# Outer-product rows on one Trainium2 core: a round of 256 adjacent batch rows, with all input loaded at the start

## The chip, the cores and the metric

The kernel runs on one core of a Trainium2 chip. The metric is the device time of one execution in microseconds (us), given as the median of several runs. Of the core's engines three matter here: VectorE (DVE in the profile) and ScalarE (ACT), which compute, and SyncE (SP), whose queue issues every transfer to the core's 16 DMA engines. The on-chip memory has 128 partitions, and a tile has one line in each.

## The reference

For each of 4096 batch rows of 256 numbers, all products of two of the row's numbers are wanted, each pair once:

```python
r_inputs: (4096, 256) float32

dot = jnp.einsum('bi,bj->bij', inputs, inputs)
iu, ju = jnp.triu_indices(d)
return dot[:, iu, ju]
```

The output has 4096 rows of 256 x 257 / 2 = 32,896 numbers (131,584 bytes a row, 539 MB in all). The input is 4.2 MB.

## The kernel before

The 4096 batch rows are worked on in 16 rounds (`groups`) of 256 rows, two rows (`REPEAT`) on each of the 128 partitions. Before the change partition p owns the 32 adjacent batch rows 32p to 32p+31, and round g takes rows 32p+2g and 32p+2g+1 from each partition (`x_in` and `x_out`). In memory the rows of neighbouring partitions are thus 32 x 131,584 bytes = 4.2 MB apart in the output.

The whole input stays in one tile `xt`, with 32 rows on each partition. It is loaded in pieces by `load` (L111 to L113), on SyncE's queue: round 0 alone (256 KB), then rounds 1 to 6 (1.5 MB), then three rounds at a time (768 KB each), called after the first piece of rounds 3, 6 and 9 (the last two lines of the loop). In the memory a partition's piece of a load is one run: 2 KB, 12 KB and 6 KB. The layer that places instructions need not keep the order of the source: the profile has the load for rounds 7 to 9 at 7.62 us, the other two at 467.5 and 706.1 us.

Within a round the 32,896 output columns are cut into five pieces of equal size (`PIECES`, in units of 64 columns). For each piece a tile `o` is taken from a pool of three (`opool`), filled and stored. A piece is a list of segments, one for each i: x[i] times x[j], for a run of j. A few of the longest go to ScalarE (L129, one instruction per row), the others to VectorE (L138, both rows in one instruction). Then SyncE issues two stores (L145), one per row, each of 128 partitions x 26,368 bytes (26,112 for the first piece of a round). The first piece of round 0 is cut into four smaller ones (`FIRST`), so that storing starts early. A tile can be filled again when both stores of the tile three pieces earlier have landed.

SyncE's queue holds loads and stores in one order: an instruction that waits there holds back those behind it.

Of the kernel before, what the change touches and what calls it, by code (L numbers as in the profile page):

```python
# [1 line left out]

# [4 lines left out]

F32 = mybir.dt.float32
AF = mybir.ActivationFunctionType
ALU = mybir.AluOpType  # L10

P = 128
UNIT = 64
REPEAT = 2
PIECES = 5
BUDGET = 0.95
AHEAD = 7
LOADED = 3
FIRST = [512, 1536, 3584]


def even_borders(lo: int, hi: int, pieces: int) -> list[int]:
    units = (hi - lo) // UNIT
    return [lo + units * c // pieces * UNIT for c in range(pieces)] + [hi]


def runs(d: int, lo: int, hi: int) -> list:


    found, at = [], 0  # L30
    for i in range(d):
        a, b = max(at, lo), min(at + d - i, hi)
        if a < b:
            found.append((i, i + a - at, a, b - a))
        at += d - i
    return found


def vector_ops(block: list) -> list:

    ops, k = [], 0
    while k < len(block):
        i, j, at, n = block[k]
        m = 2 if k + 2 < len(block) and i == j else 1
        ops.append((block[k], m))
        k += m
    return ops  # L50


def interleave(block: list) -> list:


    half = len(block)
    while half and len(vector_ops(block[:half])) > len(vector_ops(block[half:])):
        half -= 1
    a, b = vector_ops(block[:half]), vector_ops(block[half:])
    return [op for k in range(max(len(a), len(b))) for ops in (a, b) for op in ops[k : k + 1]]  # L60


def vector_time(block: list) -> float:
    return sum(68 + 1.046 * REPEAT * n * m for (*_, n), m in vector_ops(block))


def split(block: list, budget: float) -> int:


    scalar, k = 0.0, 0  # L70
    while k < len(block):
        scalar += REPEAT * (184 + 0.837 * block[k][3])
        if vector_time(block[k:]) <= budget or scalar > vector_time(block[k + 1 :]):
            break
        k += 1
    return k


def window(ap: bass.AP, free: list) -> bass.AP:
    return bass.AP(ap.tensor, ap.offset, [list(ap.ap[0]), *free])  # L80


@with_exitstack
def kernel(
    ctx: ExitStack, tc: tile.TileContext, x: bass.AP, out: bass.AP
):

    nc = tc.nc
    n, d = x.shape
    width = out.shape[1]
    assert n % (P * REPEAT) == 0 and width == d * (d + 1) // 2 and width % UNIT == 0
    groups = n // (P * REPEAT)
    borders = even_borders(0, width, PIECES)
    slot = max(b - a for a, b in zip(borders, borders[1:]))

    xpool = ctx.enter_context(tc.tile_pool(name="x", bufs=1))  # L100
    opool = ctx.enter_context(tc.tile_pool(name="o", bufs=3))

    x_in = x.rearrange("(p r) d -> p (r d)", p=P)
    x_out = out.rearrange("(p g r) c -> g p r c", p=P, r=REPEAT)


    total = n // P * d
    xt = xpool.tile([P, total + 1], F32, name="x")
    nc.vector.memset(xt[:, total:], 0.0)  # L109

    def load(g: int, end: int):  # L111
        a, b = g * REPEAT * d, end * REPEAT * d
        nc.sync.dma_start(xt[:, a:b], x_in[:, a:b])  # L113

    load(0, 1)
    load(1, AHEAD)

    for g in range(groups):
        for c, (lo, hi) in enumerate(zip(borders, borders[1:])):
            o = opool.tile([P, REPEAT, slot], F32, tag="o", name=f"o_{g}_{c}")  # L120
            first = g == c == 0
            cuts = [lo, *(FIRST if first else []), hi]
            for a, b in zip(cuts, cuts[1:]):
                block = runs(d, a, b)
                k = split(block, 0.0 if first else BUDGET * REPEAT * (b - a))
                for i, j, at, length in block[:k]:
                    for r in range(REPEAT):
                        row = (g * REPEAT + r) * d
                        nc.scalar.activation(  # L129
                            o[:, r, at - lo : at - lo + length],  # L130
                            xt[:, row + j : row + j + length],
                            AF.Copy,
                            scale=xt[:, row + i : row + i + 1],
                        )
                row = g * REPEAT * d
                for (i, j, at, length), m in interleave(block[k:]):
                    at -= lo
                    nc.vector.tensor_tensor(  # L138
                        o[:, :, at : at + m * length],
                        window(xt[:, row + j :], [[d, REPEAT], [1, m], [1, length]]),  # L140
                        window(xt[:, row + i :], [[d, REPEAT], [1, m], [0, length]]),
                        ALU.mult,
                    )
                for r in range(REPEAT):
                    nc.sync.dma_start(x_out[g][:, r, a:b], o[:, r, a - lo : b - lo])  # L145
            if c == 0 and g and g % LOADED == 0 and g - LOADED + AHEAD < groups:
                load(g - LOADED + AHEAD, min(g + AHEAD, groups))


# [1 line left out]
_INS = ["r_inputs"]  # L151
_OUTS = [((4096, 32896), "float32")]


# [20 lines left out]
```

## Time and profile before

Nine runs have a median of 1279.27 us (1278.96 to 1279.62). The profiled execution took 1279.17 us; its span, from the first to the last instruction, is 1277.4 us.

| what | value | read from |
|---|---|---|
| profiled execution, and its span | 1279.17 us, 1277.4 us | times, page |
| VectorE busy, instructions | 995.9 us (78%), 1813 | page, part 1 |
| ScalarE busy, instructions | 486.6 us (38%), 1547 | page, part 1 |
| bytes read from and written to memory | 4.19 MB, 538.97 MB | page, part 3 |
| stores of 3,296 KB and 3,264 KB | 128 and 30 issues | page, part 6 |
| loads | five: 256 KB, 1,536 KB and three of 768 KB | page, part 6 |
| VectorE waiting for stores to land | 205.5 us in 62 waits | waits |

The page divides the span into 40 equal slices and gives for each the busy share of the engines, the busy share of the 16 DMA engines in tenths (9 is 90% or more), and the GB/s that they moved. The chain of waits goes back from the last instruction to what released each step. A view by stretches gives the same for any stretch of time. Under the page lie the packet records: start, duration and size of each of the 24,624 packets that the queue's transfers were split into. A packet carries one partition's run, and 128 partitions are shared out as eight packets to each of the 16 engines.

### The profile page before, as it was taken

How to read it: one execution, taken by the hardware profiler on the slowest of the kernel's cores; microseconds unless marked ns; L12 is line 12 of the kernel's file. 1: busy time of each engine (PE TensorE's matmuls, PEld its weight loads, DVE VectorE, ACT ScalarE, POOL GpSimd, SP SyncE). 2: the span in 40 equal slices, each digit the busy share in tenths (PEclk: the TensorE clock that was granted, in tenths of full speed). 3: DMA queues.
4: the chain of work that ended last, by engine and by line, in shares of the span. 5: the costliest groups of instructions: out<-in, count | busy, mean ns of one | idle time of the engine just before them, and what ended most of it. 6: DMA issues, size and time to landing. Idle time of an engine off the chain costs nothing.

```text
span 1277.4 us, 3976 instructions
## 1 busy us (share of the span) xinstructions
DVE 995.9 (78%) x1813; ACT 486.6 (38%) x1547; POOL 0.2 (0%) x4
## 2 busy tenths in 40 slices
DVE  8997887887878777788788768788787777777770
ACT  6523434243342523424334243342523425234250
POOL 0000000000000000000000000000000000000000
DMA  8999999999999999999999999999999999999997
GB/s 357 435 428 430 435 423 434 430 426 435 427 430 431 426 434 412 429 434 432 435 432 427 422 422 433 433 431 432 433 429 434 431 427 434 429 429 433 426 433 323
DMA packets 24655, 543.43 MB, mean 425 GB/s; under 512 B 2736, under 2 KB 2736, under 8 KB 3760
## 3 DMA queue, kind: packets, MB, share of 16 engines
q1 hardware_dynamic: 24624, 543.17, 99.5%
q14 instruction: 31, 0.25, 0.0%
HBM read 4.19 MB, written 538.97 MB: 425 GB/s over the span
## 4 chain that ended last, share of the span: by engine, by line
DMA 70%; DVE 25%; SPq 1%; issue 1%; DVEq 0%
DMA out_dram<-o 70%; DVE o L138 25%; SPq L145 1%; DMA x<-in_r_inputs_dram 0%; DVEq L138 0%
## 5 line engine op out<-in xcount | busy, mean ns | idle before, releaser
L138 DVE TENSOR_TENSOR o<-x 128x356 f32<-128x356 f32 (+61 forms) x1812 | 995.8, 632 | 245.0 <-DMA out_dram<-o 205.5
L129 ACT ACTIVATE o<-x 128x253 f32<-128x253 f32 (+41 forms) x1546 | 485.3, 404 | 753.6 <-DMA out_dram<-o 744.1
L129 ACT ACT_TABLE_LOAD x1 | 1.3, 1283 | 0.7 <-PEq L162 0.7
L109 DVE MEMSET x<- 128x1 f32 x1 | 0.1, 59 | 0.8 <-PEq L162 0.8
L162 POOL MEMSET const-bfloat16-1.0<- 128x1 bf16 x1 | 0.1, 101 | 0.0
L162 POOL MEMSET const-uint8-127<- 128x1 uint8 x1 | 0.1, 101 | 0.0
L162 POOL MEMSET const-float32-0.0<- 128x1 f32 x1 | 0.1, 98 | 0.2 <-issue 0.2
L162 POOL MEMSET const-float32-1.0<- 128x1 f32 x1 | 0.1, 98 | 0.0
## 6 DMA issues: line engine op xcount, KB each, us to landing
out_dram<-o SPq DMA_DIRECT2D x128, 3296.0 KB, 29.6
out_dram<-o SPq DMA_DIRECT2D x30, 3264.0 KB, 28.6
out_dram<-o SPq DMA_DIRECT2D x2, 1472.0 KB, 11.1
x<-in_r_inputs_dram SPq DMA_DIRECT2D x3, 768.0 KB, 36.1
out_dram<-o SPq DMA_DIRECT2D x2, 1024.0 KB, 7.8
x<-in_r_inputs_dram SPq DMA_DIRECT2D x1, 1536.0 KB, 6.1
out_dram<-o SPq DMA_DIRECT2D x2, 512.0 KB, 3.8
out_dram<-o SPq DMA_DIRECT2D x2, 256.0 KB, 3.3
```

Source lines behind the costliest of these rows:

```text
L109: nc.vector.memset(xt[:, total:], 0.0)
L129: nc.scalar.activation(o[:, r, at - lo : at - lo + length], xt[:, row + j : row + j + length], AF.Copy, scale=xt[:, row + i : row + i + 1],)
L138: nc.vector.tensor_tensor(o[:, :, at : at + m * length], window(xt[:, row + j :], [[d, REPEAT], [1, m], [1, length]]), window(xt[:, row + ...
L145: nc.sync.dma_start(x_out[g][:, r, a:b], o[:, r, a - lo : b - lo])
L162: nc = _bacc.Bacc("TRN2", target_bir_lowering=False, num_devices=1)
```

## The change

A round becomes a stretch of 256 adjacent batch rows: round g holds rows 256g to 256g+255, and partition p holds rows 256g+2p and 256g+2p+1. The rows that neighbouring partitions write are then 2 x 131,584 bytes = 263 KB apart. In the input a round's 2 rows of a partition are one run of 2 KB, and different rounds of a partition are no longer adjacent. The input is loaded by three transfers ahead of the loop: round 0, rounds 1 to 7, and rounds 8 to 15. `load` and its calls in the loop go, with their constants.

```diff
-AHEAD = 7
-LOADED = 3
...
-    x_in = x.rearrange("(p r) d -> p (r d)", p=P)
-    x_out = out.rearrange("(p g r) c -> g p r c", p=P, r=REPEAT)
+    x_in = x.rearrange("(g p r) d -> p g (r d)", p=P, r=REPEAT)
+    x_out = out.rearrange("(g p r) c -> g p r c", p=P, r=REPEAT)
...
-    def load(g: int, end: int):
-        a, b = g * REPEAT * d, end * REPEAT * d
-        nc.sync.dma_start(xt[:, a:b], x_in[:, a:b])
-
-    load(0, 1)
-    load(1, AHEAD)
+    cuts = [0, 1, groups // 2, groups]
+    for a, b in zip(cuts, cuts[1:]):
+        xs = xt[:, a * REPEAT * d : b * REPEAT * d]
+        nc.sync.dma_start(xs.rearrange("p (g c) -> p g c", g=b - a), x_in[:, a:b])
...
-            if c == 0 and g and g % LOADED == 0 and g - LOADED + AHEAD < groups:
-                load(g - LOADED + AHEAD, min(g + AHEAD, groups))
```

## The prediction

> **What bounds the kernel.** I read the slices of the span first, then the queues and the chain, then the waits, then short stretches where the DMA rate dips.
>
> ```profile
> span 1277.4 us, 3976 instructions
> ...
> DVE 995.9 (78%) x1813; ACT 486.6 (38%) x1547; POOL 0.2 (0%) x4
> ...
> DMA  8999999999999999999999999999999999999997
> GB/s 357 435 428 430 435 423 434 430 426 435 427 430 431 426 434 412 429 434 432 435 432 427 422 422 433 433 431 432 433 429 434 431 427 434 429 429 433 426 433 323
> ...
> q1 hardware_dynamic: 24624, 543.17, 99.5%
> ...
> HBM read 4.19 MB, written 538.97 MB: 425 GB/s over the span
> ...
> DMA 70%; DVE 25%; SPq 1%; issue 1%; DVEq 0%
> ```
>
> The 16 DMA engines are busy from the second slice to the last but one, and nearly all bytes are output. VectorE is idle for a fifth of the span, so its 25% in the chain is time the DMA is working too. The queue's own waits say the same: SyncE mostly waits for VectorE to have something to store, while VectorE in turn waits for a store to free a buffer.
>
> ```profile
> SPq L145 <- DVE o L138: 1101.0, 83, 16.8
> ...
> DVE o L138 <- DMA out_dram<-o: 205.5, 62, 5.7
> ```
>
> So the end is set by how long the DMA engines need for their packets plus the time they stand empty. A store that VectorE finishes earlier buys nothing. The stretches show where the DMA falls below its usual rate (the last two columns are the share of the 16 engines that is busy and GB/s; a share above 1 comes from counting a packet where it starts).
>
> ```profile
> 4.00:24.00 20.00, 20.00 (x28) 15.21 (x43) 0.00 (x0) 1.00 1.00 397
> 24.00:28.00 4.00, 4.00 (x7) 0.69 (x3) 0.00 (x0) 1.00 0.56 238
> 28.00:68.00 40.00, 40.00 (x89) 20.35 (x69) 0.00 (x0) 1.00 1.01 432
> ...
> 488.00:512.00 24.00, 19.17 (x30) 6.94 (x22) 0.00 (x0) 1.00 1.01 411
> ...
> 728.00:752.00 24.00, 19.50 (x31) 6.43 (x20) 0.00 (x0) 1.00 1.01 408
> ...
> 1268.00:1276.00 8.00, 0.00 (x0) 0.00 (x0) 0.00 (x0) 1.00 0.18 76
> ```
>
> Four places lose time: the start; a hole at 24 to 28 us, where the stores of the first tile are through and the next tile's are issued only at 26.27 us; and two dips, at the loads that SyncE issues at 467.5 and 706.1 us, whose packets run some 30 us later. In the tail a few engines finish 6 to 7 us after the rest (the packet records show three, ending at 1274.5, 1274.9 and 1276.0 us, the others at 1268.5 to 1269.4).
>
> **The change part by part.** Durations are of the profiled execution, 1277.4 us of span and 1279.17 us in all; the median is 0.10 us above that.
>
> *Mid-run loads go.* The two dips cost (1 - 411/432) x 24 = 1.17 us and (1 - 408/432) x 24 = 1.33 us: their bytes are counted in the GB/s, so this is pure loss, from reads between writes. The packet records agree: 26,112-byte stores there take 1.6 to 2.0 us instead of a median 0.971. Gain 2.5 us. The two loads also leave SyncE's queue, where they hold 1.24 and 1.26 us in time in which SyncE waits for VectorE anyway; worth nothing while that wait lasts (16.8 us at its longest), and if that cover were gone 2.5 us. The third load (rounds 7 to 9) was issued at 7.62 us already, so "the last nine rounds" is six in the trace: 1.5 MB that really move.
>
> *All loads first, in 2 KB packets.* A round's rows are now 2 KB per partition in memory, so rounds 1 to 15 take 15 x 8 = 120 packets of 2 KB per engine in place of 8 of 12 KB and 24 of 6 KB. In the first load a 2 KB packet follows the one before it by 80 ns once the engine is running (84 ns long, overlapping), a 12 KB one by 457, a 6 KB one takes 234 (230 with the same overlap). So 120 x 80 = 9.6 us against 8 x 457 + 24 x 230 = 9.2: loss 0.4 us. Less mixing at the start: now loads end, then stores begin, one border instead of two or three; half of one dip's two borders is 0.6 us, today's packets before 24 us carry 1.4 us per engine over their medians, of which 0.4 is the latency of the first loads and stays. I take a gain of 0.4, with bounds of 0 and 1.0.
>
> *The hole fills.* Loads would be through at about 2.7 (first load landed) + 9.6 = 12.3 us. Behind them lie the stores of the first tile, 6.7 MB or 15.5 us at 432 GB/s, so the engines work until 27.8 us, past 27.1 us where the packets of the next tile's stores begin today. Gain 0.44 x 4 = 1.76 us. By engine the hole is 0.45 to 2.6 us in the packet records; the engine that ends last decides, so these are the bounds. What is late next: the first tile's buffer comes free about 1.5 us later, but VectorE wants it only after its third tile (stored at 38.6 us), 10 us of cover; without that cover VectorE would start late by that 1.5 us, and the DMA still would not run dry, having two tiles queued.
>
> *Issue on SyncE.* Two loads of 896 and 1024 packets now stand before the first store, ready at 4.81 us. No row has such an issue. A 128-packet one takes 0.38 to 0.42 us on an empty queue and up to 1.26 us on a full one. If it grows with packets, that is 15 x 0.42 = 6.3 us (SyncE free at 7.4) or 15 x 1.26 = 18.9 (free at 20.0). VectorE and ScalarE depend on the first load alone and keep computing. I take the short end, since these are issued on an empty queue, as its row is: nothing lost, for the load packets run until 12.3 us.
>
> *Addresses.* Neighbouring partitions write 263 KB apart instead of 4.2 MB, with the same packets: 16,384 of 26,368 bytes, 3,840 of 26,112. Per engine that is 1,024 and 240. The trace has no other spacing, so the price is bounded by its rows. Medians are 978 and 971 ns, means 982.4 and 979.9, so today's disturbance is 4.4 x 1,024 + 8.9 x 240 = 6.6 us. If the new spacing removed it: -6.6 us. If every packet took what the slowest tenth takes today (989 and 981): 13.7 - 6.6 = +7.0 us. If stores ran as the mixed stretch at 411 GB/s does: 5% or some 60 us. I take 0: the nearest row is the same store at its usual pace, 978 ns with 975 the shortest, which looks like the engines' own limit rather than the memory's.
>
> The Trainium skill has a rule that speaks against the change. "DMA: Bandwidth & Descriptors", section Latency and other measured facts, reports copies slowed by power-of-two spacing of partition rows: full speed (214 GB/s each way) at 4 MiB plus 4 KiB, 103 at plain 4 MiB, 207 at 512 KiB, and a pad of 192 bytes not helping. The spacing before is 4 MiB plus 16 KiB, and its 978 ns agree with full speed; the new one is 256 KiB plus 1 KiB, which the page does not have. By its nearest line, 207 of 214, the stores would take 3.4% longer, an estimate of about +42 us and 1317 in place of the sum below.
>
> *Unchanged:* computing, store count, the three late engines of the tail.
>
> Sum: -2.5 + 0.4 - 0.4 - 1.8 + 0 = -4.3 us. 1279.17 - 4.3 = 1274.9; the median's 0.1 us does not matter. That is -0.34%; about 0.2%, or 2.6 us, can be told from no change.
>
> **The rivals.**
>
> *Stores get slower by their spacing.* Place: every 26 KB packet. 4.3 us over 1,264 packets is 3.4 ns: a mean of 985.8 ns for the large ones gives the whole gain back, and beyond 987.9 ns the kernel is slower by over 0.2%. With all packets at today's slowest tenth the time is 1274.9 + 7.0 = 1281.9. For it: the margin is tiny, and in the stretch from 30 to 480 us, where the engines run most in step, packets exceed the median by 2.6 us per engine, against 0.2 us from 505 to 700. Against: the packets sit at one duration in all rounds.
>
> *The issue holds the first stores.* SyncE free at 20.0 us, stores done 15.5 us later at 35.5 in place of 27.1: +8.4, less the 3.7 us of load time that no longer comes later (16 packets x 230 ns) and the 2.5 of the dips: +2.2, 1281.4. For it: 1.2 us issues are common. Against: in the trace those come with several transfers queued ahead.
>
> *The gain is hidden.* The engine that ends last had the smallest hole (0.45 us), and mixing at the start grows to what one dip costs (1.3 lost in place of 0.4 gained): -2.5 + 0.4 + 1.3 - 0.45 = -1.3, 1277.9, no change. For it: only the last engine counts. Against: the three late ones fell behind gradually, after the hole.
>
> *Spacing helps.* Today's disturbance goes too: 1274.9 - 6.6 = 1268.3. For it: quiet stretches exist. Against: nothing ties them to addresses.
>
> **How the numbers follow.** Forecast 0.42; spacing helps 0.09; hidden 0.10; issue 0.09 (0.04 of it within 0.2%); slower stores 0.30 (0.03 of it within 0.2%). Faster 0.51, same 0.17, slower 0.32. The forecast's own range is 1273.5 to 1276.6 by the bounds of hole and mixing. The range runs from 1269, leaving out some 0.05 of the helped cases, to 1290, 12 ns more per packet than forecast, leaving out about half of the slower stores, 0.15.
>
> **What would show it.** No dips in mid-run and no hole at 24 to 28 us; three input issues before the first store; input packets over by 13 us; large packets still at 978 ns median and 982 mean; the tail as before. Wrong if that mean is above 986, if the first store's packets start after 14 us with idle engines before them, or if VectorE waits for anything but stores.

## The result, and the profile after

The changed kernel takes 1275.13 us (median of 10 runs, 1274.73 to 1276.16), the kernel before 1279.19 us. The ratio is 0.9969, with a 95% interval from 0.9961 to 0.9976: faster by 4.1 us, or 0.3%. The forecast was 1274.9 us.

The page of the changed kernel, its slices, queue, bytes and chain:

```profile
span 1273.1 us, 3975 instructions
...
DVE 996.1 (78%) x1813; ACT 486.7 (38%) x1547; POOL 0.2 (0%) x4
...
DMA  9999999999999999999999999999999999999998
GB/s 380 431 432 434 425 435 425 436 424 435 428 433 425 434 425 435 424 435 426 435 427 432 429 431 425 435 428 431 428 433 428 432 430 431 425 434 426 435 426 353
...
q1 hardware_dynamic: 26000, 543.17, 99.8%
...
HBM read 4.19 MB, written 538.97 MB: 427 GB/s over the span
...
DMA 70%; DVE 25%; issue 1%; SPq 1%; DVEq 0%
```

It is the same kernel with the same bound: the same bytes, the same chain, the DMA engines full. What is gone is the 412 GB/s slice of before, and the first slice moves 380 instead of 357 GB/s. The stretches in which before lost time (columns as before: stretch, length, busy time by engine, clock, DMA share, GB/s):

```profile
4.00:24.00 20.00, 18.52 (x26) 15.40 (x44) 0.00 (x0) 1.00 1.02 401
24.00:28.00 4.00, 4.00 (x7) 0.00 (x0) 0.00 (x0) 1.00 1.02 436
28.00:68.00 40.00, 40.00 (x89) 21.05 (x70) 0.00 (x0) 1.00 1.01 434
488.00:512.00 24.00, 20.87 (x32) 8.75 (x27) 0.00 (x0) 1.00 1.02 437
728.00:752.00 24.00, 19.09 (x32) 5.78 (x18) 0.00 (x0) 1.00 1.02 437
1264.00:1272.00 8.00, 0.00 (x0) 0.00 (x0) 0.00 (x0) 1.00 0.36 155
```

The hole at 24 to 28 us (0.56 of the engines busy before) is full, and both dips (411 and 408 GB/s before) are at 437. In the first line VectorE has lost 1.48 us of work, which it had not lost before; its rows in order of time (start, length, what, and in brackets the idle time ahead of it and what ended that):

```profile
3.62 4.28 DVE L133 TENSOR_TENSOR o<-x 128x512 f32<-128x512 f32 x9 [2.76 <-DMA x<-in_r_inputs_dram]
9.38 50.72 DVE L133 TENSOR_TENSOR o<-x 128x988 f32<-128x988 f32 x84 [1.48 <-DMA x<-in_r_inputs_dram]
```

In round 0 VectorE waits twice for input: for round 0's own load, and at 7.9 us for the second load, whose last engine lands at 9.35 us. The source of the second wait is in the code: where one instruction covers two segments (m = 2), the second is one number shorter but is read at full length, so it reads one number past the end of its row, which behind a partition's second row is round 1's first. The instruction that waits (the first of the 128x988 group, 2 x 2 x 247 numbers) is the first of round 0 with m = 2. Before, the load with round 1 had landed at 7.25 us, in time.

Where the 4.3 us of span went is best read round by round, in one profile of each kernel. In the records each store has 16 landings, one per DMA engine. They do not name the engines: below, the last engine is the one that lands last, and the middle engine is the median of the 16. From the landing of a round's last store on the last engine to that of the round before (us; round 0 from the start of the span):

| kernel | round 0 | round 6 | round 9 | rounds 7, 8 and 10 | end |
|---|---|---|---|---|---|
| before | 91.00 | 82.44 | 82.31 | 78.50, 78.55, 77.70 | 1276.40 |
| changed | 93.13 | 78.53 | 78.59 | 78.72, 78.84, 78.45 | 1272.20 |

Round 0 is 2.1 us longer, since it now has all input; rounds 6 and 9 are 3.9 and 3.7 us shorter, their input and dips being gone; of these 7.6 us, 1.25 are given back in rounds 7, 8 and 10 (0.75 of it in round 10, which was quicker than the usual 78.5 before). The other rounds differ by 0.05 us in sum. 2.13 - 7.63 + 1.25 + 0.05 = -4.20, of the 4.3 us of span.

### The profile page after: what moved, and what is told of

Read it like the earlier page. It is cut to its first block, busy times and chain, and to the rows that moved or that the text cites. A ratio compares the mean times of both kernels' runs of the same rounds, so it can differ in the third digit from the quotient of the medians.

```text
span 1273.1 us, 3975 instructions
## 1 busy us (share of the span) xinstructions
DVE 996.1 (78%) x1813; ACT 486.7 (38%) x1547; POOL 0.2 (0%) x4
## 4 chain that ended last, share of the span: by engine, by line
DMA 70%; DVE 25%; issue 1%; SPq 1%; DVEq 0%
DMA out_dram<-o 70%; DVE o L133 25%; SPq L140 1%; DMA x<-in_r_inputs_dram 1%; DVEq L133 0%; SPq L111 0%
## 6 DMA issues: line engine op xcount, KB each, us to landing
x<-in_r_inputs_dram SPq DMA_DIRECT2D x1, 2048.0 KB, 13.5
out_dram<-o SPq DMA_DIRECT2D x2, 512.0 KB, 11.1
out_dram<-o SPq DMA_DIRECT2D x2, 256.0 KB, 10.6
```

## The experiments

**Spacing and load time apart.** The change does two things at once: it spreads stores differently, and it moves the loads. Three kernels fill the square.

The changed loads with the old spacing:

```diff
-    x_out = out.rearrange("(g p r) c -> g p r c", p=P, r=REPEAT)
+    x_out = out.rearrange("(p g r) c -> g p r c", p=P, r=REPEAT)
```

> The changed kernel with one line put back: the stores go to the old addresses, 4.2 MB apart per partition, while the input stays as changed. The products of each row are unchanged, but they are written to other rows of the output, so only the spacing of the stores differs from the changed kernel. Theory A (the time of the loads is everything, the spacing nothing): 1275.1 us within 0.5, an undisturbed round 78.33 us between the median landings of its last stores, 26,368-byte packets at a median of 978 to 981 ns. Theory B (the new spacing brings part of the gain): slower than the changed kernel by 1 us or more, 1276 to 1279, with more excess per packet. Theory C (the new spacing costs something that the loads' gain covers): faster than the changed kernel, 1271 to 1274.

Measured: 1274.95 us (1274.79 to 1275.01), ratio to before 0.9967 [0.9954, 0.9979]. Large packets have a median of 982 ns (981 in the changed kernel) and a mean of 983.9 (983.7). Going from 4.2 MB to 263 KB is worth nothing either way. Theory A.

The old rows and spacing with all input first:

```diff
-    load(1, AHEAD)
+    load(1, groups // 2)
+    load(groups // 2, groups)
...
-            if c == 0 and g and g % LOADED == 0 and g - LOADED + AHEAD < groups:
-                load(g - LOADED + AHEAD, min(g + AHEAD, groups))
```

> The kernel before with one thing changed: all input is loaded ahead of the loop in three transfers (rounds 0, 1 to 7, 8 to 15), rows and spacing as before, so that a partition's piece of a load is one run of 2, 14 or 16 KB. Theory A: the whole gain and a little more, since large packets cost 0.4 us less: 1274.7 us, rounds 6 and 9 at 78.3 us instead of 81, no hole at 24 to 28 us. Theory B: part of the gain is missing, 1276 to 1279.

Measured: 1274.22 us (1274.16 to 1274.35), ratio 0.9961 [0.9948, 0.9975]. Theory A. This is the change without its new rows, and it is the fastest kernel of this study that computes the whole result. A second set of runs:

> The kernel with all input loaded first and old rows and spacing once more, to set it against the changed kernel's 1275.1 us with more runs: 1274.2 us again if its 0.9 us are real; 1275 us if the first five runs were lucky. Theory for the difference: input packets of 14 and 16 KB cost 0.4 us less than those of 2 KB, and the loads land 0.6 to 1.2 us sooner.

Measured: 1274.26 us (1274.19 to 1274.37), ratio 0.9962 [0.9950, 0.9975]; the slowest of its ten runs is below the fastest of the changed kernel (1274.73). In the first set's profile its input lands on the last engine at 13.98 us instead of 15.13.

The new rows and spacing with the loads at their old times:

```diff
+AHEAD = 7
+LOADED = 3
...
-    cuts = [0, 1, groups // 2, groups]
-    for a, b in zip(cuts, cuts[1:]):
+    def load(a: int, b: int):
         xs = xt[:, a * REPEAT * d : b * REPEAT * d]
         nc.sync.dma_start(xs.rearrange("p (g c) -> p g c", g=b - a), x_in[:, a:b])
+    load(0, 1)
+    load(1, AHEAD)
...
+            if c == 0 and g and g % LOADED == 0 and g - LOADED + AHEAD < groups:
+                load(g - LOADED + AHEAD, min(g + AHEAD, groups))
```

> The changed kernel's rows and spacing with the loads at the times of the kernel before (rounds 0, 1 to 6, then three rounds at a time in mid-run). Theory A: as the kernel before plus some 0.2 us for the smaller packets, 1279.4 us, with rounds 6 and 9 at 81 us and the hole at 24 to 28 us. Theory B: faster than the kernel before by 1 us or more though the loads stay in mid-run, 1275 to 1278.

Measured: 1279.87 us (1279.59 to 1280.54), ratio 1.0006 [0.9997, 1.0015]: as before, 0.5 us above theory A's 1279.4. The hole and the dips are back; its stretches:

```profile
24.00:28.00 4.00, 4.00 (x7) 0.38 (x2) 0.00 (x0) 1.00 0.64 270
488.00:512.00 24.00, 19.12 (x30) 7.48 (x23) 0.00 (x0) 1.00 1.02 410
728.00:752.00 24.00, 19.45 (x30) 7.09 (x22) 0.00 (x0) 1.00 0.99 399
```

and the same stretches with the old rows and all input first (its second set of runs):

```profile
24.00:28.00 4.00, 4.00 (x6) 0.00 (x0) 0.00 (x0) 1.00 0.99 424
488.00:512.00 24.00, 20.87 (x32) 8.27 (x26) 0.00 (x0) 1.00 1.00 429
728.00:752.00 24.00, 18.08 (x30) 5.79 (x18) 0.00 (x0) 1.00 1.00 428
```

| | loads in mid-run | all loads first |
|---|---|---|
| rows 4.2 MB apart, large input packets | 1279.19 (before) | 1274.24 |
| rows 263 KB apart, 2 KB input packets | 1279.87 | 1275.13 (changed) |

Down each column the new rows cost 0.7 to 0.9 us; along each row the earlier loads gain 4.7 to 5.0 us. With the old spacing but 2 KB packets the time was 1274.95, so most of that column's 0.9 us belongs to the way the input is loaded, not to the stores. Whether it is the 2 KB packets or the order in which the rows are read was not tested apart.

**The new wait.** Round 1 gets a load of its own, so that the number past the row is there early:

```diff
-    cuts = [0, 1, groups // 2, groups]
+    cuts = [0, 1, 2, groups // 2, groups]
```

> The changed kernel with round 1 loaded by a transfer of its own, so that VectorE, whose last product of a row with two segments reads one number past the row into round 1, need not wait for the 1.8 MB load. The 1.48 us wait of VectorE at 7.9 to 9.4 us should go. Theory A (the DMA engines set the end and have loads to move until 14 us): no change, 1275.1 us within 0.5. Rival (the wait delays stores that the DMA engines then lack): faster by up to 1.5 us, 1273.7.

Measured: 1275.71 us (1274.96 to 1277.66), ratio 0.9975 [0.9965, 0.9985]. VectorE's wait is gone: in its rows one group runs from 3.47 us without a break.

```profile
3.47 37.16 DVE L133 TENSOR_TENSOR o<-x 128x512 f32<-128x512 f32 x51 [2.62 <-DMA x<-in_r_inputs_dram]
```

The time did not fall: it is 0.6 us above 1275.1, just outside theory A's 0.5, and the rival's 1273.7 is not reached. Taking the wait away brought nothing back; the middle engine ends at 1267.25 us, as in the changed kernel (1267.17). The extra transfer is not neutral, though: in this profile the last of the input lands on the last engine at 17.0 us instead of 15.1, and after round 0 that engine is 2.3 us behind the middle one instead of 0.75. Why is not shown.

**What a mid-run load costs beyond its bytes.** First the loads of before cut finer:

```diff
-LOADED = 3
+LOADED = 1
```

> The kernel before with the mid-run loads cut finer: one round (256 KB) at each of rounds 1 to 9 in place of three rounds at rounds 3, 6 and 9, the same bytes. It tells whether a mid-run load costs by its borders or by its bytes. By its borders (1.3 us each beyond its bytes, as in the two dips): some eight loads in mid-run in place of two, 1287 us. By its bytes: as before, 1279.2 us.

Measured: 1280.66 us (1280.47 to 1281.12), ratio 1.0011 [1.0002, 1.0021]. Eight loads were issued in mid-run. Rounds 2 to 9 take 79.67 us on average on the last engine, 1.1 us more than the 78.6 of an ordinary round; 0.6 of that is bytes. So a load of 256 KB costs 0.5 us beyond its bytes there, not 1.3: the theory of the borders is wrong by 6 us in the total, that of the bytes by 1.5. On the middle engine the same rounds take 78.97 us, and 0.6 us over the usual 78.33 is the bytes alone.

Then loads of three sizes on top of the kernel with all input first:

```diff
+AGAIN = {5: 1, 8: 3, 11: 8}
...
+            if c == 0 and g in AGAIN:
+                load(0, AGAIN[g])
```

> All input loaded ahead of the loop with the old rows and spacing (1274.2 us), and then rounds already used are loaded once more into their own place: 256 KB (2 KB packets) at round 5, 768 KB (6 KB) at round 8, 2 MB (16 KB) at round 11. Results are unchanged. Bytes alone cost 0.6, 1.8 and 4.9 us. By borders, each load costs 1.3 us beyond its bytes: the three rounds in which the packets run are longer by 1.9, 3.1 and 6.2 us. By bytes, beyond-cost 0.4, 1.3 and 3.4: longer by 1.0, 3.1 and 8.3 us. If the rounds after a load run quicker, as those after the two dips did (77.8 us in place of 78.3), about 0.5 to 1.5 us comes back each time; the total is 1283 to 1287 us either way.

Measured: 1284.22 us (1283.36 to 1285.0), ratio 1.0038 [1.0023, 1.0053], 10.0 us over the kernel without them, of which 7.3 us are bytes. By round, against the same round without the load:

| load | round | last engine, us longer | beyond its bytes | middle engine, us longer | beyond its bytes |
|---|---|---|---|---|---|
| 256 KB | 5 | 1.2 | 0.6 | 0.8 | 0.2 |
| 768 KB | 8 | 3.8 | 2.0 | 2.5 | 0.7 |
| 2 MB | 11 | 6.9 | 2.0 | 6.3 | 1.4 |

Neither theory holds over the whole range: the loss grows from the small load to the middle one, and on the last engine no further. Which property of a load sets it (packet size changed with the size here) stays open. What comes back afterwards is seen on the middle engine: the three rounds after the 2 MB load take 77.84 us each instead of 78.33. At the end the middle engine is 7.5 us later than without the three loads (1273.92 instead of 1266.44), which is their bytes, and the last engine 10.6 (1282.15 instead of 1271.51): only the late engines keep what a load costs beyond its bytes.

**How much spacing could have cost.** Stores at exact powers of two; the last 128 columns are not stored:

```diff
-                    nc.sync.dma_start(x_out[g][:, r, a:b], o[:, r, a - lo : b - lo])
+                    e = min(b, WIDTH)
+                    at = g * REPEAT * WIDTH + r * WIDTH + a
+                    to = bass.AP(out.tensor, out.offset + at, [[PITCH, P], [1, e - a]])
+                    nc.sync.dma_start(to, o[:, r, a - lo : e - lo])
```

with WIDTH = 32768 numbers and PITCH = 32 x WIDTH (4 MiB); in the second kernel PITCH = 2 x WIDTH (256 KiB) and a round starts at g x 128 x PITCH.

> The changed kernel with its stores placed exactly 4 MiB apart from partition to partition (rows 131,072 bytes apart inside); the last 128 of the 32,896 columns of each row are not stored, and rows lie at other addresses, so the stores carry 0.4% fewer bytes. It measures how much the spacing of stores could cost at all. If the engines are the limit whatever the spacing: 26,368-byte packets at a median of 978 to 982 ns and 1275.1 - 4.8 = 1270.3 us. If exact power-of-two spacing makes the memory the limit: packets well above 982 ns; at twice their time 2500 us.

Measured: 1701.3 us (one run). Its page:

```profile
span 1699.5 us, 3975 instructions
...
DMA  9999999999999999999999999999999999999996
GB/s 214 348 358 374 384 385 385 372 366 347 358 337 317 305 322 325 329 318 312 300 318 316 299 266 315 335 326 294 286 309 319 306 295 293 307 292 280 314 327 188
```

The engines are as busy as ever and move a quarter less: a busy share says nothing of how long a packet takes. The 26,368-byte packets have a median of 1271 ns (978 at the shortest, 2746 at the longest) instead of 981.

> The same with the stores exactly 256 KiB apart, in stretches of 256 adjacent rows as in the changed kernel; the last 128 columns of each row are not stored. If the extra 1 KiB per partition of the changed kernel's spacing was what kept it at full speed, packets are well above 982 ns here and the time above 1280 us; if 256 KiB spacing is harmless by itself, 978 to 982 ns and 1270.3 us.

Measured: 1270.36 us (one run), the 1270.3 of harmless spacing; packets at a median of 982 ns.

```profile
span 1268.6 us, 3975 instructions
...
GB/s 374 430 431 431 429 430 430 429 431 430 431 429 431 428 431 427 433 427 434 426 434 428 431 427 433 426 434 429 431 428 431 429 432 426 434 430 430 431 428 355
```

So for these stores spacing is no small matter at 4 MiB sharp, and none at 4 MiB plus 16 KiB (before), 256 KiB plus 1 KiB (changed) or 256 KiB sharp. The Trainium skill's page "DMA: Bandwidth & Descriptors", section Latency and other measured facts, has full speed at 4 MiB plus 4 KiB and about half at 4 MiB, for copies: its direction holds here, with three quarters of full speed for this kernel instead of half (319 of 427 GB/s on the pages). The prediction's estimate from its 207 of 214 at 512 KiB, 1317 us, did not come true: at 256 KiB, which the page does not have, nothing is lost.

**The late engines.** ScalarE gets one instruction for both rows of a segment, on the kernel with all input first:

```diff
-                    for r in range(REPEAT):
-                        row = (g * REPEAT + r) * d
-                        nc.scalar.activation(
-                            o[:, r, at - lo : at - lo + length],
-                            xt[:, row + j : row + j + length],
+                    row = g * REPEAT * d
+                    nc.scalar.activation(
+                        o[:, :, at - lo : at - lo + length],
+                        window(xt[:, row + j :], [[d, REPEAT], [1, length]]),
```

> All input loaded first, old rows and spacing (1274.2 us), with one ScalarE instruction for both rows of a segment in place of two: the second row is multiplied by the first row's number, so the second row's products of ScalarE's segments are not the reference's, and ScalarE has 773 products in place of 1546. Theory: the three DMA engines that end 4 to 5 us after the others are those that also fetch instructions (31 fetches of 8 KB in the run, about 0.4 to 0.6 us of delay each). Then there are about 25 fetches, one of the three late engines loses about half of its lag, and the time falls only if that engine is the last: 1272 to 1274.2 us. Rival (the lag belongs to the engines themselves): three engines as late as before and 1274.2 us.

Measured: 1273.81 us (1273.04 to 1273.94), ratio 0.9959 [0.9944, 0.9974]. Its page:

```profile
span 1271.3 us, 3121 instructions
...
q14 instruction: 24, 0.20, 0.0%
```

and the same lines with one ScalarE instruction per row (all input first, second set):

```profile
span 1272.6 us, 3975 instructions
...
q14 instruction: 31, 0.25, 0.0%
```

Seven fetches of instructions fewer. All four runs are faster than the ten without the edit, but the profiled one is the fastest of the four (1273.04 us, the others 1273.79 to 1273.94), so the lags of its trace may be smaller than usual. The last three engines land at 1268.3, 1268.8 and 1270.4 us, the other 13 at 1266.0 to 1267.1. With 31 fetches (all input first, second set) they land at 1269.5, 1270.6 and 1271.7, the others at 1265.8 to 1266.9. Against the middle engine, 1266.5 and 1266.3 us, the three lags sum to 8.0 instead of 12.9 us, so 0.7 us for each fetch left out in this pair of profiles. The landing records show it fetch by fetch. In the changed kernel, after round 0, the summed lag of the three rises by more than 0.3 us from one store to the next in 25 places, and each time a fetch lies between the two landings or within 3 us of them; of the 29 fetches, one has no such rise near it. The rises add up to 23.6 us, 0.8 for each fetch, and about half of that is made up for in between. In the kernel with half the ScalarE instructions there are 22 such rises and 22 fetches. The fetches delay the three engines; but all three gained, not one, so they are not tied one to an issuing engine as the theory had it.

## Why the prediction was right

*The bound* was read rightly: only DMA time counted. VectorE's new wait of 1.48 us for input, which the forecast had not seen and which was one of its own signs of being wrong, did not show in the time.

*Mid-run loads.* Forecast were 2.5 us beyond 3.7 us of bytes, 6.2 in all. The rounds 6 and 9 became 7.6 us shorter, less 1.25 given back later: 6.4. That the term came out well is luck: the stretches at 411 and 408 GB/s give the mean engine, while the last engine loses more in a dip and the middle ones recover afterwards; neither of these two was in the working. On the middle engine nothing of the 2.5 us is left at the end: rounds 6 and 9 became 5.46 us shorter, rounds 7, 8, 10 and 11 1.7 us longer, and the difference is the bytes.

*Loads first, the hole, small packets.* Forecast for round 0 was +3.7 + 0.4 - 0.4 - 1.76 = +1.9; measured +2.1. In its parts: on the last engine the first tile's last store lands 3.74 us later (30.74 instead of 27.00; forecast 3.7), and the next store follows in 7.8 instead of 9.2 us, so the hole was worth 1.4 there, within 0.45 to 2.6. The two terms of 0.4 cancel in the sum; no run tells them apart. That the new rows' packets cost 0.4 us agrees with the 0.7 to 0.9 between the rows of the square only in direction.

*The clock times on the way were too early.* Input was to be over by 12.3 us and the first tile's stores by 27.8; they landed at 14.3 (middle engine; 15.1 on the last) and 30.7. The 120 packets took 11.1 us on the middle engine, 92 ns each instead of the 80 taken from the first load. The sum did not use these times, only that they lie past the old hole, and later was safer. But the first tile's buffer came free 3.7 us later, not 1.5; VectorE's third tile was stored only at 40.37 us, so 9.6 us of cover were left.

*Issue.* The 896- and 1024-packet loads took SyncE 0.42 and 0.56 us, where the lower bound had 2.9 and 3.4. In these issues on an empty queue the time hardly grows with the packets (128 take up to 0.42 us); this rival is gone.

*Addresses.* Zero was taken, and the old spacing under the changed loads made 0.2 us, which is within the spread of the runs. Large packets had a median of 981 and a mean of 983.7 ns, a little above the 978 and 982 of the forecast and below its limit of 986. The rival of slower stores, given 0.30, and that of helpful spacing both fall for these two spacings. That the mechanism exists, the 4 MiB kernel shows.

*What failed* is the step "unchanged: the three late engines of the tail", and with it a sum made alike for all engines. The middle engine gained 1.9 us (1269.07 to 1267.17), the last one 4.2. On the middle engine rounds 6 and 9 of before were 5.5 us longer than the usual 78.33, 3.7 of them bytes, and the 1.8 beyond the bytes came back in rounds 7, 8, 10 and 11, which took 77.83 to 78.10 us. The late engines lost more and kept it: the last one's lag behind the middle one grew by 1.5 and 1.1 us in those two rounds, against 0.2 each now, and ended at 7.3 us before and 5.0 in the changed kernel. Had the lag stayed as it was, the end would have come 1.9 us earlier, not 4.2. The last engine sets the end, and its loss in the dips happens to be near the mean that the stretches gave: the total was right to 0.2 us, by luck, with this step wrong.

## What to carry to other kernels

Where transfers set the time, account for it round by round on the last engine: moved bytes come back where they are moved to, and what is left over are holes and mixed stretches. Loads that fit a hole at the start cost less there than between stores, even in 2 KB packets. When a change does two things, run the square: here the part that the change is named for was worth nothing, and the part that came with it all of the gain, so that doing it alone was the better kernel by 0.9 us.

## What was not expected of the hardware

After a mixed stretch the stores run faster than usual: 77.83 us a round on the middle engine for one to three rounds, instead of 78.33, with packets nearer 968 and 978 ns. That the engines are then out of step is a guess; no run set their steps apart by itself. Three of the 16 DMA engines end 2 to 8 us after the middle one in every kernel that stores at full speed, and their lag goes with the instructions fetched (8 KB, 309 ns a fetch): a fetch raises their summed lag by about 0.8 us, and with all input first about half of that is made up for before the end, so that 31 fetches leave 12.9 to 13.5 us. And stores exactly 4 MiB apart moved 319 GB/s over the span, in place of 427, with the DMA share still at 9 tenths or more until the last slice.
